# Turning tokens by TensorE transposes in a two-layer cross-attention kernel on one core

## The chip, the core and the metric

The kernel runs on one NeuronCore of a Trainium2 chip. The core has a matrix engine (TensorE, in the profile PE, its weight loads PEld), a vector engine (VectorE, DVE), a scalar engine (ScalarE, ACT), a general engine (GpSimd, POOL) and an engine that issues DMAs (SyncE, SP). TensorE multiplies a stationary operand (at most 128 by 128, loaded first) with a moving one and writes to PSUM, which has eight banks of 128 partitions by 512 fp32 values. [...]

The metric is the device time of one execution in microseconds (us). It is compared as a median over runs.

## The reference

Two layers work on `x` (8 batches, 512 tokens, 256 channels) with a context (8, 512, 128). Each layer adds an attention and then a feed-forward to `x`, each behind a layer norm:

```python
x = x + _L0_xattn_ref(_layernorm(x), ctx, ...)   # causal self-attention + cross-attention, 16 heads of 16
x = x + _L0_ffn_ref(_layernorm(x), ...)          # 1024 wide, rows quantised to 127 steps, ternary weights
x = x + _L1_xattn_ref(_layernorm(x), ctx, ctx, ...)  # cross-attention, 16 heads of 16
x = x + _L1_ffn_ref(_layernorm(x), ...)          # 1024 wide, one scale for the whole tensor and each weight
```

In layer 0, `y` is the sum of a causal attention of the tokens with themselves and an attention of the tokens to the context, projected by one matrix. The last feed-forward quantises its whole input with one scale, `max(|x|) / 127` over all batches, so it can't start before the last batch's layer norm is done.

## The kernel before

**Units.** The attentions are cut into 24 units: causal self-attention (S), cross-attention of layer 0 (C) and cross-attention of layer 1 (X) for each of 8 batches. A unit has 512 queries, 512 keys and 16 heads. Scores, exponentials and value products run in fp32. Scores are made twice: once with queries in rows, from which VectorE takes each row's maximum (`MATMUL pair<-qk`, then `TENSOR_REDUCE mx<-pair`), and once with keys in rows, from which ScalarE makes the exponentials (`MATMUL bank<-qk`, `ACTIVATE p<-bank`). The value products (`MATMUL bank<-p,v`) take these.

**Tilings of the array.** The score products use 48 or 50 rows of a half of the array (48\*128 and 50\*128 in the profile, in pairs side by side; planner mode "rows"). The value products and all projections use 32 columns at a time, four side by side (128\*32, mode "cols"). Some products use the whole array (128\*128, mode "full").

**Token turns.** Before each projection, tokens have to be turned, so that channels lie on partitions. `ln_job` (line 494 on) loads 512 tokens as a tile `xa` of 128 partitions by 4 token blocks by 256 channels, normalises them, and then, for each half `k` of the channels, multiplies four blocks of 128 by 128 with the identity into one PSUM bank. The function `wide` cuts each of these products into four of 32 columns. ScalarE or VectorE copies the bank into `xlt`, from which the query, key and value projections read. There are 16 such layer norms (8 batches of S, 8 of X; units C take the S tokens again), so 32 banks. An fp32 product appears in the trace as two records.

**The last heads.** `last_heads_job` (line 931 on) ends the last unit without the trip through memory that the other units take: the two last groups of heads are copied from their value bank to `ol`, turned to token order (`MATMUL bank<-ident_r,ol`), divided by their sums into `ytok`, and turned back (`MATMUL bank<-ident_r,ytok`). `last_proj_job` makes the last projection, the statistics and the last layer norm from it.

**The last feed-forward's first inputs.** `turn_job` (line 1032 on) turns the first three batches (`TURNED = 3`) of the last feed-forward's input, `y4`, two banks of four blocks each (`MATMUL bank<-ident_r,y`), as soon as the last projection's products are planned; ScalarE copies the banks back over the tile. Batch 0 is then quantised by ScalarE (one half, `ACTIVATE y<-y,magic,sc_x`) and VectorE (the other half) once the scale `sc_x` is known.

**Order.** No loop runs over units. All the work is written as jobs (Python generators), and a planner, `Plan`, keeps a clock for each engine, advances it by a price for each instruction, and picks the next piece of TensorE work: a maximum step, an exponential step, a value step, or a part of a job, by readiness, priority and how much work ScalarE and VectorE still have queued. The order in which instructions are then issued on every engine, on SP's DMA queue and on POOL too, is fixed at build time. Each engine runs its list in that order and waits where a semaphore says so. TensorE's price is this:

```python
def pe(self, cols, mode="full"):
    if mode != self.mode:
        self.clock["pe"] += SWITCH          # 0.165
        self.mode = mode
    self.clock["pe"] += max(cols / 2415, cols / 2165 - 0.08) if mode == "cols" else 0.008 + cols / 2340
```

PSUM banks are handed out by hand. All products go through a wrapper, `Writer` (line 250 on), whose `matmul` makes the first write of a new use of a bank wait for the last readers of the old one. All products are therefore recorded at one line, L259, and the other engines' operations on banks at L241.

Of the kernel before, what the change touches and what calls it, by code (L numbers as in the profile page):

```python
# [16 lines left out]
NB, T, C, CC, H, D, FF = 8, 512, 256, 128, 16, 16, 1024  # L17
P = 128
# [58 lines left out]
class Plan:  # L77
# [39 lines left out]
    def op(self, kind, n, *deps):  # L117
        fixed, rate = RATE[kind]
        return self.run(kind.rstrip("2"), fixed + n * rate, *deps)

    def dma(self, kb, *deps, dims=2, rate=195):
        t = self.run("sp", 0.33 if dims == 2 else 0.65, *deps)
        self.clock["dma"] = max(self.clock["dma"], t + 0.95) + kb / rate
        return self.clock["dma"] + 0.35

    def until(self, *keys):
        while not all(k in self.at for k in keys):
            yield self.now + 0.2
        t = max((self.at[k] for k in keys), default=0.0)
        if t + LAT > self.now:  # L130
            yield t + LAT
        return t

    def take(self, tag):
        ring = self.rings[tag]
        while not ring:
            yield self.now + 0.2
        t = heapq.heappop(ring)
        if t + LAT > self.now:
            yield t + LAT  # L140
        return t
# [108 lines left out]
class Writer(Readers):  # L250
# [5 lines left out]
        self.tc = tc  # L256

    def matmul(self, out, *args, **kw):
        r = self.eng.matmul(out, *args, **kw)  # L259
        name = out.tensor.name  # L260
        for i in self.of[name]:
            if self.last[i][0] != name:
                for reader in self.last[i][1]:
                    self.tc.add_manual_dep(r.ins, reader.name, SYNC, reason="bank")
                self.last[i] = (name, [])
        return r
# [20 lines left out]
def build(tc, A, out):  # L287
    nc = Engines(tc)
# [8 lines left out]
    plan = Plan()  # L297
# [3 lines left out]
    def tile(tag, shape, dtype, name, pool=wp):  # L301
        return pool.tile(shape, dtype, tag=tag, name=name, bufs=BUFS[tag])
# [15 lines left out]
    def wide(out, lhs, rhs, start=True, stop=True):  # L318


        for c in range(0, P, 32):
            nc.tensor.matmul(out[c : c + 32], lhs[:, c : c + 32], rhs, start=start, stop=stop)

    def pe_next(t=None):

        return (plan.now if t is None else t + LAT, 1.0)
# [19 lines left out]
    ident = ident_r.bitcast(F32)  # L346
# [122 lines left out]
    def stats(x, nm):  # L469

        st = wp.tile([P, NT, 6], F32, tag="bnst", name=f"st_{nm}", bufs=3)
        mv = wp.tile([P, NT, 2], F32, tag="bnmv", name=f"mv_{nm}", bufs=3)
        r = wp.tile([P, NT], F32, tag="rstd", name=f"r_{nm}", bufs=3)
        neg = wp.tile([P, NT], F32, tag="nmean", name=f"nm_{nm}", bufs=3)
        for t in range(NT):
            nc.vector.bn_stats(st[:, t, :], x[:, t, :])
            op("dve", C)
            yield plan.now + 0.4
        for t in range(NT):
            nc.vector.bn_aggr(mv[:, t, :], st[:, t, :])  # L480
        te = plan.run("dve", 0.4)
        nc.gpsimd.tensor_scalar(r, mv[:, :, 1], LN_EPS, 0.0, ALU.add, ALU.add)
        nc.gpsimd.tensor_tensor(r, r, mhalf, ALU.pow)
        nc.gpsimd.tensor_scalar(neg, mv[:, :, 0], -1.0, 0.0, ALU.mult, ALU.add)
        te = plan.run("pool", 1.3, te)
        return mv[:, :, 1], neg, r, te

    def normalise(dst, src, nm, r, t):

        nc.gpsimd.tensor_scalar(dst, src, nm[:, t : t + 1], 1.0, ALU.add, ALU.mult)  # L490
        nc.gpsimd.tensor_scalar(dst, dst, r[:, t : t + 1], 0.0, ALU.mult, ALU.add)
        return plan.run("pool", 0.95)

    def ln_job(key, src, nm, n_uses):

        if key[0] == "X":
            yield from until(("x3", key[1]))
        if key == ("S", 0):
            x = first_x
            yield at["x0"] + LAT  # L500
        else:
            yield from take("xa")
            x = tile("xa", [P, NT, C], F32, f"xa_{nm}")
            nc.sync.dma_start(x, src())
            yield dma(512) + LAT
        var, neg, r, te = yield from stats(x, nm)
        yield te
        for t in range(NT):
            if key == ("S", 0):
                at["first"] = nc.vector.tensor_scalar(  # L510
                    x[:, t, :], x[:, t, :], neg[:, t : t + 1], r[:, t : t + 1], ALU.add, ALU.mult
                ).ins.name
                te = op("dve2", C, te)
            else:
                te = normalise(x[:, t, :], x[:, t, :], neg, r, t)
        yield from take("xlt")
        xlt[key] = tile("xlt", [P, 2, T], F32, f"xlt_{nm}")
        uses[key] = [n_uses, 0.0]
        for k in range(2):
            yield pe_next(te)  # L520
            ps, pb = yield from gen_bank()
            for t in range(NT):
                wide(ps[:, t * P : (t + 1) * P], x[:, t, k * P : (k + 1) * P], ident)
            tm = plan.pe(4 * T, "cols")
            tm = evacuate(xlt[key][:, k, :], ps, T, tm)
            give_bank(pb, tm)
        give("xa", tm)
        at[key] = tm
# [402 lines left out]
    def last_heads_job():  # L931
        key = ("X", NB - 1)
        yield from until(("y", *key, 0))
        yt = y_t[key]
        yield from take("rb")
        ytok = tile("rb", [P, T], F32, "ytok").rearrange("p (t h d) -> p t h d", t=NT, d=D)
        for i, G in enumerate((NG - 2, NG - 1)):
            yield from take("oc")
            yield from until(("av", G))
            o = tile("oc", [P, T], F32, f"ol{i}")  # L940
            bank = av_t.pop(G)
            t = evacuate(o, banks[bank], T)
            plan.bank_give("av", bank, t)
            yield pe_next(t)
            ps, pb = yield from gen_bank()
            for k in range(NT):
                nc.tensor.matmul(ps[:, k * P : (k + 1) * P], o[:, k * P : (k + 1) * P], ident, start=True, stop=True)
            t = plan.pe(4 * T)
            give("oc", t)
            ps4 = ps.rearrange("p (t h r) -> p t h r", t=NT, h=4)  # L950
            rz = wp.tile([P, 32], F32, tag="zr", name=f"rz{i}", bufs=2)[:, :16].rearrange("p (t h) -> p t h", t=NT)
            nc.vector.reciprocal(rz, ps4[:, :, :, D])
            plan.run("dve", 0.3, t)
            nc.vector.tensor_tensor(
                ytok[:, :, 4 * i : 4 * i + 4, :], ps4[:, :, :, :D], rz.unsqueeze(3).broadcast_to([P, NT, 4, D]), ALU.mult
            )
            t = op("dve", 256)
            give_bank(pb, t)
        yield pe_next(t)
        ps, pb = yield from gen_bank()  # L960
        for k in range(NT):
            nc.tensor.matmul(
                ps[:, k * P : (k + 1) * P], ytok[:, k].rearrange("p h d -> p (h d)"), ident, start=True, stop=True
            )
        t = plan.pe(4 * T)
        at["yl"] = evacuate(yt[:, 1], ps, T, t)

    def last_proj_job():
# [63 lines left out]
    def turn_job():  # L1032

        yield from until(("acc", 1))
        for b in range(TURNED):
            y = early["y4"][b]
            yield plan.now
            for k in range(2):
                yield pe_next()
                ps = yield from gen_bank()  # L1040
                for t in range(NT):
                    yield pe_next()
                    nc.tensor.matmul(
                        ps[0][:, t * P : (t + 1) * P], y[:, t, k * P : (k + 1) * P], ident, start=True, stop=True
                    )
                    plan.pe(T)
                if k == 0:
                    first = ps
            for k, (bank, i) in enumerate((first, ps)):
                nc.scalar.copy(y[:, 2 * k : 2 * k + 2].rearrange("p t c -> p (t c)"), bank)  # L1050
                give_bank(i, op("act", T))
# [400 lines left out]
    while plan.jobs or a < len(AV_STEPS):  # L1452
# [24 lines left out]
        if any(can.values()):  # L1477
            k = min(urgent)[1] if urgent else "e" if closing and can["e"] else "a" if can["a"] else min((feed[k], k) for k in "me" if can[k])[1]
# [74 lines left out]
    cols = iter(range(64))  # L1553
# [40 lines left out]
    for bs in ((0,), (1,), (2, 3), (4, 5), (6, 7)):  # L1594
# [3 lines left out]
        for f in range(8):  # L1598
            i = 8 * b + n * f
            ps = [banks[2 + i % 6]] if n == 1 else [pairs[1 + f % 3][:, x] for x in range(2)]  # L1600
# [86 lines left out]
    for i in range(2 * NB):  # L1687
# [4 lines left out]
        ps = half_ps.pop(i, None)  # L1692
        if ps is None:
            ps = bias_first(i)

        for j in range(16):
            f, t = (j // 2, j % 2) if i == 0 else (j % 8, j // 8)
# [76 lines left out]
```

## Time and profile before

| | |
|---|---|
| median of 3 runs | 1463.38 us |
| all runs | 1459.09, 1463.38, 1472.07 us |
| span of the profiled execution, first to last instruction | 1458.4 us |
| instructions in it | 36089 |
| mean granted TensorE clock | 0.971 |
| first token turns | 9.16 to 12.57 us |
| last exponentials done; last value product done | 1358.35; 1361.74 us |
| last feed-forward, from its first product | 1377 to 1458 us |

The profile is of one execution; the page shows its span, and its own device time is not listed beside it. The median of the runs is 5.0 us above the span. A line of the groups names the source line, the engine, the operation, output and inputs by the program's names, shapes and the number of instructions; after the bar stand the total busy time in us, the mean of one instruction in ns, and the engine's idle time before them with what ended it. A line of the timeline gives the start in us, the length in us, and the same names; in square brackets stands the idle time of the engine before it.

The stretches of the run, as busy us of each engine with the number of instructions, then the granted clock, the DMA share and GB/s:

```
100.00:400.00 300.00, 291.24 (x3286) 126.17 (x3290) 236.29 (x326) 212.16 (x412) 148.15 (x207) 0.99 0.58 136
400.00:700.00 300.00, 291.66 (x3396) 126.55 (x3393) 249.65 (x364) 219.11 (x411) 160.44 (x239) 0.99 0.64 148
700.00:1000.00 300.00, 288.03 (x3216) 123.52 (x3208) 235.54 (x328) 216.18 (x410) 144.94 (x215) 0.97 0.60 139
1000.00:1340.00 340.00, 324.14 (x2992) 123.35 (x2984) 283.47 (x360) 260.06 (x493) 151.53 (x238) 0.98 0.59 146
1340.00:1380.00 40.00, 36.94 (x213) 19.32 (x212) 13.62 (x42) 24.55 (x46) 9.70 (x18) 0.89 0.26 95
```

The engines in each row are TensorE's products, its weight loads, VectorE, ScalarE and GpSimd.

### The profile page before, as it was taken

What the parts mean: (1) busy time and instruction counts of PE and PEld (TensorE: products, weight loads), DVE (VectorE), ACT (ScalarE), POOL (GpSimd) and SP (SyncE); (2) the same over time, 40 slices, a digit from 0 to 9 for tenths busy, and PEclk for the clock granted to TensorE, in tenths of its full rate; (3) what the DMA queues carried; (4) which work ended last, traced back from release to release, by engine and by line L of the source; (5) the groups of instructions that cost most, each with busy time, mean ns of one, the idle gap of its engine ahead of it and who ended that gap; (6) DMA issues with size and microseconds to landing.
All of it is one profiled execution on the core that took longest, in us unless ns stands there. A gap on an engine that the chain in (4) does not pass through costs nothing. (4 is left out here: it accounts for less than half of the span.)

```text
span 1458.4 us, 36089 instructions
## 1 busy us (share of the span) xinstructions
PE 1374.8 (94%) x14400; PEld 597.5 (41%) x14400; DVE 1142.0 (78%) x1591; ACT 1035.5 (71%) x1904; POOL 681.6 (47%) x1025
## 2 busy tenths in 40 slices
PE   4999999999999999999999999999999998999978
PEld 2443444444444444434344433443333333333527
DVE  4678588697788886898777996689899888766397
ACT  1456767677768867767677777668778795777587
POOL 1463355465455465464653552654455541524332
PEclk8899999999999999999899999999999999999899
DMA  6593565667576755665457655556647657373343
GB/s 126 152 216 76 133 139 125 142 138 182 132 161 150 161 129 141 156 161 126 105 126 155 163 126 132 142 120 160 163 105 169 155 149 196 105 176 110 117 142 116
DMA packets 155612, 207.03 MB, mean 142 GB/s; under 512 B 71940, under 2 KB 74244, under 8 KB 154932
## 3 DMA queue, kind: packets, MB, share of 16 engines
q1 hardware_dynamic: 155444, 204.73, 58.0%
q8 instruction: 113, 1.85, 0.5%
q14 instruction: 55, 0.45, 0.1%
HBM read 68.15 MB, written 47.43 MB: 79 GB/s over the span
## 5 line engine op out<-in xcount | busy, mean ns | idle before, releaser
L241 DVE TENSOR_REDUCE mx<-pair 128x2 f32<-128x1024 f32 (+3 forms) x768 | 808.9, 1086 | 210.7 <-PE pair L259 194.6
L241 ACT ACTIVATE p<-bank 128x512 f32<-128x512 f32 (+1 forms) x1408 | 712.0, 587 | 232.7 <-PE bank L259 224.8
L259 PE MATMUL bank<-p,v 128*32 128x512 f32 (+3 forms) x3072 | 371.7, 563 | 2.9 <-DVE mrow L241 1.3
L259 PE MATMUL bank<-qk 50*128 50x512 f32 (+3 forms) x1536 | 337.6, 433 | 16.2 <-ACT p L241 8.0
L259 PE MATMUL pair<-qk 48*128 48x512 f32 (+3 forms) x1536 | 325.5, 438 | 25.7 <-DVE mx L241 11.8
L259 PEld LDWEIGHTS bank<-qk 50*128 50x128 f32 x1536 | 159.6, 190 | 215.7 <-ACT p L241 142.9
L259 PEld LDWEIGHTS pair<-qk 48*128 48x128 f32 x1536 | 148.0, 191 | 171.5 <-DVE mx L241 83.4
L384 POOL TENSOR_SCALAR qkt<-qkt 128x512 fp32r<-128x512 f32 x92 | 57.1, 621 | 164.1 <-ACT qkt L241 157.5
L241 ACT ACTIVATE qkt<-bank,qk_bias 128x512 f32<-128x512 f32 x96 | 66.6, 693 | 81.0 <-PE bank L259 65.4
L409 POOL TENSOR_TENSOR qkt<-qkt 128x512 fp32r<-128x512 f32 x92 | 118.8, 1291 | 7.7
L259 PEld LDWEIGHTS bank<-p,v 128*32 128x32 f32 x3072 | 70.9, 109 | 114.6 <-issue 85.9
L384 POOL TENSOR_SCALAR mhl<-mx 128x32 fp32r<-128x32 f32 x48 | 11.8, 245 | 171.3 <-DVE mx L241 164.8
L883 POOL TENSOR_TENSOR yt<-oc,rb 128x512 f32<-128x512 f32 x31 | 39.8, 1283 | 73.3 <-DMA rb<-scrz 50.9
L259 PE MATMUL pair<-mask,ident 64*128 64x128 bf16 (+2 forms) x768 | 58.0, 226 | 6.9 <-DVE mx L241 4.7
L259 PE MATMUL bank<-ident,mask 64*128 64x64 bf16 (+1 forms) x768 | 52.7, 206 | 3.7 <-ACT p L241 1.2
L259 PEld LDWEIGHTS <-ident 64*128 64x128 bf16 x768 | 26.1, 97 | 71.0 <-issue 52.8
L259 PEld LDWEIGHTS <-mask 64*128 64x128 bf16 x768 | 25.8, 96 | 69.3 <-issue 61.0
L241 ACT COPY v<-bank 128x512 f32<-128x512 f32 x44 | 26.2, 596 | 39.4 <-PE bank L259 39.1
L241 ACT COPY ev<-bank 128x512 f32<-128x512 f32 x56 | 33.5, 598 | 17.9 <-PE bank L259 17.9
L241 DVE SCALAR_TENSOR_TENSOR h<-bank,so,bc_l_b 128x512 f32<-128x512 f32 x64 | 45.3, 741 | 0.9 <-PE bank L259 0.7
L241 ACT ACT_TABLE_LOAD x34 | 43.6, 1283 | 1.9 <-PEq L1762 0.7
L1189 POOL TENSOR_SCALAR h<-h,sh 128x1024 f32<-128x1024 f32 x32 | 36.0, 1125 | 17.7 <-DVE sh L241 15.2
(230 smaller groups left out, 1686.4 us busy)
## 6 DMA issues: line engine op xcount, KB each, us to landing
qk<-qkt SPq DMA_DIRECT2D x288, 256.0 KB
scro<-ev SPq DMA_DIRECT2D x94, 256.0 KB
oc<-scro SPq DMA_DIRECT2D x47, 256.0 KB
rb<-scrz SPq DMA_DIRECT2D x47, 256.0 KB
x_d<-xb SPq DMA_DIRECT2D x15, 512.0 KB
xa_s<-in_x SPq DMA_DIRECT2D x8, 512.0 KB
xb<-in_x SPq DMA_DIRECT2D x8, 512.0 KB
xr<-x_d SPq DMA_DIRECT2D x16, 256.0 KB
```

What stands on the lines that cost most here:

```text
L241: r = f(*args, **kw)
L259: r = self.eng.matmul(out, *args, **kw)
L384: nc.gpsimd.tensor_scalar(dst, src, 1.0, 0.0, ALU.mult, ALU.add)
L409: nc.gpsimd.tensor_tensor(dst, full, high.bitcast(F32), ALU.subtract)
L883: nc.gpsimd.tensor_tensor(y, o, rb, ALU.mult)
L1189: nc.gpsimd.tensor_scalar(ht, ht, s[:, t - t0 : t - t0 + 1], MAGIC, ALU.mult, ALU.add)
```

## The change

Wherever a block of 128 by 128 was multiplied by the identity to turn it (token turns, the last heads both ways, the last feed-forward's first inputs), the kernel calls TensorE's transpose with the same operands instead. The token turns, which were four products of 32 columns for each block, become one transpose of 128 by 128 for each block. `Writer` gets a `transpose` next to `matmul`, with the same waits for banks. The planner's prices change with it: a bank of four blocks is priced at 512 columns in place of 2048, and a single block in `turn_job` at 128 in place of 512. The token turns keep the mode "cols" in the planner's price. The other products with the identity, among them the row maxima's, the one that adds the residual in `last_proj_job` and `all_max`, stay.

```diff
--- before.py
+++ after.py
@@ -256,7 +256,12 @@
         self.tc = tc
 
     def matmul(self, out, *args, **kw):
-        r = self.eng.matmul(out, *args, **kw)
+        return self.writes(out, self.eng.matmul(out, *args, **kw))
+
+    def transpose(self, out, *args):
+        return self.writes(out, self.eng.transpose(out, *args))
+
+    def writes(self, out, r):
         name = out.tensor.name
         for i in self.of[name]:
             if self.last[i][0] != name:
@@ -520,8 +525,8 @@
             yield pe_next(te)
             ps, pb = yield from gen_bank()
             for t in range(NT):
-                wide(ps[:, t * P : (t + 1) * P], x[:, t, k * P : (k + 1) * P], ident)
-            tm = plan.pe(4 * T, "cols")
+                nc.tensor.transpose(ps[:, t * P : (t + 1) * P], x[:, t, k * P : (k + 1) * P], ident)
+            tm = plan.pe(T, "cols")
             tm = evacuate(xlt[key][:, k, :], ps, T, tm)
             give_bank(pb, tm)
         give("xa", tm)
@@ -944,8 +949,8 @@
             yield pe_next(t)
             ps, pb = yield from gen_bank()
             for k in range(NT):
-                nc.tensor.matmul(ps[:, k * P : (k + 1) * P], o[:, k * P : (k + 1) * P], ident, start=True, stop=True)
-            t = plan.pe(4 * T)
+                nc.tensor.transpose(ps[:, k * P : (k + 1) * P], o[:, k * P : (k + 1) * P], ident)
+            t = plan.pe(T)
             give("oc", t)
             ps4 = ps.rearrange("p (t h r) -> p t h r", t=NT, h=4)
             rz = wp.tile([P, 32], F32, tag="zr", name=f"rz{i}", bufs=2)[:, :16].rearrange("p (t h) -> p t h", t=NT)
@@ -959,10 +964,8 @@
         yield pe_next(t)
         ps, pb = yield from gen_bank()
         for k in range(NT):
-            nc.tensor.matmul(
-                ps[:, k * P : (k + 1) * P], ytok[:, k].rearrange("p h d -> p (h d)"), ident, start=True, stop=True
-            )
-        t = plan.pe(4 * T)
+            nc.tensor.transpose(ps[:, k * P : (k + 1) * P], ytok[:, k].rearrange("p h d -> p (h d)"), ident)
+        t = plan.pe(T)
         at["yl"] = evacuate(yt[:, 1], ps, T, t)
 
     def last_proj_job():
@@ -1040,10 +1043,8 @@
                 ps = yield from gen_bank()
                 for t in range(NT):
                     yield pe_next()
-                    nc.tensor.matmul(
-                        ps[0][:, t * P : (t + 1) * P], y[:, t, k * P : (k + 1) * P], ident, start=True, stop=True
-                    )
-                    plan.pe(T)
+                    nc.tensor.transpose(ps[0][:, t * P : (t + 1) * P], y[:, t, k * P : (k + 1) * P], ident)
+                    plan.pe(P)
                 if k == 0:
                     first = ps
             for k, (bank, i) in enumerate((first, ps)):
```

## The prediction

> **What bounds the kernel now.** I read the page's busy table and slices first, then the groups of TensorE instructions by shape, then TensorE's timeline round single token turns, and last the waits and the timeline of the end.
>
> ```profile
> PE 1374.8 (94%) x14400; PEld 597.5 (41%) x14400; DVE 1142.0 (78%) x1591; ACT 1035.5 (71%) x1904; POOL 681.6 (47%) x1025
> PE   4999999999999999999999999999999998999978
> PEclk8899999999999999999899999999999999999899
> ```
>
> TensorE is in the top tenth in nearly every slice, at a granted clock of 0.9 or more after the first 70 us. Busy time of pipelined products overlaps, so I asked who waits for whom. The waits say the same: ScalarE's exponentials waited 224.8 us for TensorE and VectorE's maxima 194.6 us, while TensorE's own longest totals are 16.5 us (for VectorE's maxima) and 9.8 us (for the exponentials). From some 30 us to 1340 us the kernel is bound by TensorE's stream, and what leaves that stream shortens the run, unless it uncovers another wait. The chain that ended last reaches back to 1377 us only and says nothing of this middle.
>
> The groups that change, by shape (mean ns of one record stands after the bar's comma):
>
> ```profile
> L259 PE MATMUL bank<-ident_r,xa_s 128*32 128x128 f32 x512 | 18.3, 291 | 9.2 <-DVE xa_s L241 9.2
> L259 PE MATMUL bank<-ident_r,xa_x 128*32 128x128 f32 x512 | 18.1, 285 | 0.0
> L259 PE MATMUL bank<-ident_r,y 128*128 128x128 f32 x48 | 5.5, 275 | 0.0
> L259 PE MATMUL bank<-ident_r,ol 128*128 128x128 f32 x16 | 2.2, 281 | 0.0
> L259 PE MATMUL bank<-ident_r,ytok 128*128 128x128 f32 x8 | 1.1, 275 | 0.0
> ```
>
> An fp32 product is two records: 16 layer norms, two halves, 16 products of 32 columns make 1024 records. The token turns are 36.4 us of busy time, everything else that changes is 8.8 us.
>
> **Pitch of a token turn.** Not the busy time but the distance to the next group's start is what a group costs. TensorE's timeline (start, us, group):
>
> ```profile
> 510.00 1.06 PE L259 MATMUL bank<-p,v 128*32 128x512 f32 x8
> 511.00 0.23 PE L259 MATMUL bank<-ident,mask 64*128 64x64 bf16 x4
> ...
> 512.18 1.07 PE L259 MATMUL bank<-xlt_s,w_Sq 128*32 128x512 f32 x8
> 513.06 1.06 PE L259 MATMUL bank<-ident_r,xa_x 128*32 128x128 f32 x32
> 514.05 0.73 PE L259 MATMUL pair<-qk 48*128 48x512 f32 x4
> 514.71 1.08 PE L259 MATMUL bank<-ident_r,xa_x 128*32 128x128 f32 x32
> 515.61 1.04 PE L259 MATMUL bank<-xlt_s,w_Sq 128*32 128x512 f32 x8
> ```
>
> The group at 513.06 costs 0.99 us (a row-tiled score group, 48*128, follows), the one at 514.71 costs 0.90 (a 32-column group follows). A 32-column group of the same work costs 512.18 to 513.06 = 0.88 before another 32-column group and 510.00 to 511.00 = 1.00 before a row-tiled one. So leaving one tiling of the array for another costs 0.12 us.
>
> I read the timeline round all turns. Apart from the two at the start (9.16 us), there are 30; 11 have a 32-column group before them and 2 behind; all other neighbours are row-tiled.
>
> **Pitch after.** A turn becomes four 128 by 128 transposes. No transpose stands in this trace. The nearest rows are full-array fp32 products of the same size:
>
> ```profile
> 350.07 0.49 PE L259 MATMUL bank<-ident_r,l1w1s 128*128 128x128 f32 x2
> 350.49 0.26 PE L259 MATMUL pair<-mask,ident 64*128 64x128 bf16 x4
> ...
> 1369.40 5.54 PEld L259 LDWEIGHTS bank<-ident_r,y 128*128 128x128 f32 x48
> ```
>
> 48 weight loads of 128 fp32 columns take 5.54 us, 0.115 each, with the products beside them. I take one load and one product for a transpose, bound by the load: 4 x 0.115 = 0.46. The fixed part: two records cost 0.42 between row-tiled groups (350.07 to 350.49); less 2 x 0.115 that leaves 0.19 for the first load and the way out. A turn then costs 0.65.
>
> - Between row-tiled groups: 0.99 - 0.65 = 0.34 saved; 30 x 0.34 = 10.2 us.
> - With a 32-column group before: the change of tiling is new, 11 x 0.12 = 1.3 us lost. Behind: 2 x 0.09 (0.90, not 0.99, was paid before) = 0.2 lost.
> - Sum 8.7 us. TensorE has little idle time between 100 and 1340 us (busy 291 of 300 us in such windows), so I let 8 us through: about a tenth is eaten where the next group waits for VectorE or ScalarE anyway.
>
> Bounds of the price. Low: an fp32 product takes its pair of records, 0.23 us; a quarter of it would be 0.0575, 4 x 0.0575 + 0.19 = 0.42, saving 0.57 x 30 - 1.5 = 15.6 us. High: nothing overlaps and each transpose shows the full 275 ns of one record: 4 x 0.275 + 0.19 = 1.29, a loss of 0.30 x 30 + 1.5 = 10.5 us. I take the load's rate because 48 loads of this very shape were streamed so, and neither end was seen.
>
> The Trainium skill speaks against the change here ("TensorE: Matmul & The Clock Gate", Part 4): a transpose takes about 275 ns in a kernel, and does not count as activity for the clock gate. By its price the sum would be the loss of the high end, some 10 us. The trace can't show a transpose; what it shows of the clock is 0.97 to 0.99 over the windows from 100 to 1340 us, and a turn of 0.65 us comes once in some 45 us.
>
> The same rule of exclusion decides the tiling: the skill ("TensorEngine Tiling (Array Packing)", Gotcha 2) says that column tiling and fp32 transposes exclude each other. No run here shows it.
>
> **Start.** The first two turns reach from 9.16 to 12.57 us, where the first query product starts. VectorE's last token tile ends at 10.08, and ScalarE's copy of half 0 starts at 11.16. With transposes half 0 is done some 0.3 us after 10.08, half 1 0.46 later: the query product could start near 11.0, 1.5 earlier. Behind it lie the second half's weights, whose DMA lands near 14.7, and from 19 to 27 us the stacking DMAs of queries and keys. Between 0 and 1.5 I take 1.0.
>
> **End.** After the last value product (1361.7) the chain runs through two head turns and the token-order turn, then the projection, the statistics and the input scale:
>
> ```profile
> 1363.52 1.05 PE L259 MATMUL bank<-ident_r,ol 128*128 128x128 f32 x8
> 1364.41 1.02 PE L259 MATMUL bank<-xb,ident_r 128*128 128x512 f32 x2
> ...
> 1374.73 1.07 ACT L241 COPY y<-bank 128x512 f32<-128x512 f32 x2 [0.71 <-PE bank L259]
> 1375.82 1.28 ACT L241 ACT_TABLE_LOAD   x1
> ```
>
> Two of the turns (the second head group, and the one from token order back) lie on it: 8 records to 4, 0.46 each, 0.9 together. Then ScalarE waits 0.64 and 0.71 us for the y turns before it copies them; the table load (1.28) and the first quantising step (1377.22) are behind those copies, while the scale that it needs is ready at 1376.1. The 24 y turns fall from 5.5 to 2.8 us, the copies close up, and the step then starts when the scale is there: 1.1 more. Sum 2.0; bounds 0 (the copies are late for another reason) and 2.5.
>
> **What moves.** The program's order is made by a planner from prices. A token turn's price falls from 0.866 (2048 columns) to 0.212 (512), 32 times, 20.9 us of planned TensorE time, against my 0.65 a piece. So the plan, close to the chip before (0.866 to 0.90-0.99), becomes optimistic at these points, and everything behind them, on all engines and on SP's and POOL's queues (loads, stacking, row DMAs, normalising), may stand in another order. No added wait, DMA or instruction is visible in the edit. I price the new order at 0, and give it 6 us either way: as the waits of TensorE in the middle sum to about 45 us, that is an eighth of them.
>
> **Sum.** 8 + 1 + 2 = 11 us from the span of 1458.4: 1447.4. The median of the runs is 1463.4, 5.0 above the span; added back, 1452.
>
> **Rivals.**
> 1. *Transposes run at the quarter price.* 15.6 + 1.5 + 2.5 = 19.6, so 1444. For it: the change's own prices assume it. Against: the load's rate of 0.115.
> 2. *The new order adds TensorE waits.* The plan thinks TensorE earlier than it is, puts score groups before VectorE has freed their banks (today 30 such waits, 16.5 us, and 18 for the exponentials, 9.8), and the in-order stream stops. With the 45 us up by half, 1452 + 22 = 1474, slower. It decides from 11 us of added waits on (no gain left), and passes 1% slower from 26. For it: nothing in the edit re-tunes the planner's other constants. Against: banks and buffers are as before and the plan knows real bank releases through the same rules.
> 3. *A transpose is no faster than the product* (the high end): 10.5 lost in the turns and about 1 at the end: 1475.
> 4. *Nothing is gained because VectorE takes over*: it is at 78%, so 11 us less leave it at 79%; I give it no share of its own.
>
> **Numbers.** Forecast (order within 6 us, price near the load's rate) 0.52, range 1446 to 1458. Rival 1: 0.22. Rival 2: 0.18. Rival 3: 0.08. Range 1438 (rival 1 with 6 us from the order) to 1469 (inside rival 2). A measurement of this kernel tells about 1% (14.6 us) from no change. Faster by more (under 1448.7): rival 1 nearly whole, and a quarter of the forecast: 0.34. Slower by more (over 1478): half of rival 2 and a little of rival 3: 0.11. Between: 0.55.
>
> **What would show it.** TensorE records fall from 14400 to 13468 if a transpose is one record (896 + 12 + 24 fewer). Turn pitch in the timeline: 0.65 right, 0.42 rival 1, over 1.0 rival 3. TensorE's waits for maxima and exponentials: unchanged right, up by over 10 us rival 2. The first query product near 11 us, the y copies without gaps. The forecast is wrong if turns are short and the span does not fall: then the waits must have grown by as much.

## The result and the profile after

The changed kernel takes 1524.21 us (median of 4 runs, 1516.70 to 1533.17) against 1462.34 us before: 1.0417 times the time before, 95% interval 1.0364 to 1.0469. The forecast was 1452 us in a range of 1438 to 1469. It missed, on the wrong side.

The page of the kernel after: busy table, then the slices of TensorE and of its granted clock.

```profile
PE 1397.8 (92%) x13468; PEld 587.9 (39%) x13468; DVE 1139.6 (75%) x1576; ACT 1041.9 (68%) x1919; POOL 678.9 (45%) x1025
PE   5999999999998998998999999899899999899878
PEclk8899999999998998998999999999899999899899
```

There are 13468 TensorE records, as forecast: 932 fewer, since a transpose leaves one record. Yet TensorE's busy time has grown by 23.0 us and its idle time from 83.6 to 126.6 us (span less busy). The slices show both: eights stand now in the middle of the TensorE row, and more of them than before in that of the clock. The mean granted clock of the profile fell from 0.971 to 0.939.

The transposes themselves, by shape, and TensorE's timeline round two turns:

```profile
L262 PE MATMUL bank<-ident_r,xa_s 128*128 128x128 f32 x64 | 11.0, 305 | 9.4 <-DVE xa_s L241 9.2 <-ACT p L241 0.2
L262 PE MATMUL bank<-ident_r,xa_x 128*128 128x128 f32 x64 | 10.9, 303 | 0.7 <-POOL xa_x L496 0.7
L262 PE MATMUL bank<-ident_r,y 128*128 128x128 f32 x24 | 2.9, 275 | 0.0
L262 PE MATMUL bank<-ident_r,ol 128*128 128x128 f32 x8 | 1.3, 280 | 0.0
L262 PE MATMUL bank<-ident_r,ytok 128*128 128x128 f32 x4 | 0.6, 272 | 0.0
```

```profile
66.90 0.48 PE L259 MATMUL bank<-qk 50*128 50x512 f32 x2
67.31 0.66 PE L262 MATMUL bank<-ident_r,xa_s 128*128 128x128 f32 x4
67.90 0.85 PE L259 MATMUL bank<-p,v 128*32 128x384 f32 x8
68.68 0.30 PE L259 MATMUL bank<-ident_r,mhl 64*16 64x64 f32 x8
68.91 0.66 PE L262 MATMUL bank<-ident_r,xa_s 128*128 128x128 f32 x4
69.50 0.64 PE L259 MATMUL bank<-p,v 128*32 128x256 f32 x8
```

A turn costs 67.31 to 67.90, 0.59 us, where the forecast had 0.65 and the old one 0.99. The busy time of all that was changed fell from 45.2 (36.4 + 8.8) to 26.7 us. So the turns are not the loss: without them TensorE's busy time grew by 23.0 + 18.5 = 41.5 us, at a lower clock, and its idle time by 43.0.

TensorE's waits (us in total, times, longest), three of before first, then the longest after:

```profile
PE pair L259 <- DVE mx L241: 16.5, 30, 1.6
PE bank L259 <- DMA qk<-mrow: 4.6, 2, 2.7
PE bank L259 <- DVE am L241: 1.8, 1, 1.8
```

```profile
PE pair L259 <- DVE mx L241: 32.6, 48, 2.3
PE bank L259 <- DMA qk<-mrow: 12.9, 5, 7.2
PE bank L259 <- ACT p L241: 12.7, 29, 1.6
PE pair L259 <- DMA qk<-qkt: 11.3, 6, 7.3
PE bank L259 <- DVE am L241: 9.5, 3, 5.4
```

Waits for VectorE's maxima doubled, from 16.5 us to 32.6; those for the DMAs of the maxima rows rose from 4.6 to 12.9, those for `am` (the maxima by which a feed-forward quantises) from 1.8 to 9.5. One of the waits for rows, on SP's queue (its DMA issues, with the time they held the queue) and on TensorE:

```profile
583.33 5.19 SPq L612 DMA_DIRECT2D qk<-qkt  x6
588.62 1.46 SPq L746 DMA_DIRECT2D qk<-mrow  x2
```

```profile
586.62 0.38 PE L259 MATMUL pair<-qk 48*128 48x256 f32 x2
594.24 1.41 PE L259 MATMUL bank<-qk 50*128 50x512 f32 x2 [7.23 <-DMA qk<-mrow]
```

Six stacking DMAs of 256 KB stand on SP ahead of the two 16 KB DMAs with the maxima rows, without which the next exponential group can't start. TensorE stands for 7.23 us. The stretches round it (busy us and instructions of TensorE, its loads, VectorE, ScalarE and GpSimd, then granted clock, DMA share, GB/s) show what follows:

```profile
582.10:585.50 3.40, 3.40 (x72) 2.46 (x72) 2.89 (x5) 1.59 (x4) 1.04 (x1) 1.00 0.29 68
585.50:588.90 3.40, 1.41 (x14) 0.40 (x12) 2.24 (x4) 0.58 (x1) 0.00 (x0) 0.99 1.00 193
588.90:602.50 13.60, 8.26 (x62) 3.94 (x62) 2.45 (x2) 4.45 (x8) 0.51 (x2) 0.50 0.80 154
602.50:606.00 3.50, 3.50 (x46) 1.69 (x46) 2.40 (x6) 3.03 (x8) 0.31 (x1) 1.00 0.23 81
```

After a stretch of 3.4 us in which TensorE worked for 1.41, its clock is halved for 13.6 us, and its products take about twice as long in them (eight value products of 512 columns took 1.93 us in a half-clock piece of before, at 1354.57 us, and 1.06 outside it, at 1349.28). A wait can thus be paid twice. Over the run, the clock stood at one half in 12 pieces and 85.3 us before, in 27 pieces and 184.6 us after; this is called half-clock time below. TensorE's busy time inside these pieces was 74.0 us before and 159.6 after. At half speed, half of the 85.6 us added is stretch: 42.8 us, which accounts for the 41.5.

### The profile page after: what moved, and what is told of

The parts are those of the page before. It is cut to its first block, busy times and chain, and to the rows that moved or that the text cites. A ratio compares the mean times of both kernels' runs of the same rounds, so it can differ in the third digit from the quotient of the medians.

```text
span 1524.4 us, 34236 instructions
## 1 busy us (share of the span) xinstructions
PE 1397.8 (92%) x13468; PEld 587.9 (39%) x13468; DVE 1139.6 (75%) x1576; ACT 1041.9 (68%) x1919; POOL 678.9 (45%) x1025
## 4 chain that ended last, share of the span: by engine, by line
PE 63%; DVE 11%; DMA 10%; ACT 7%; POOL 4%; issue 3%; SPq 2%; POOLq 0%; ACTq 0%; DVEq 0%
PE bank L259 49%; PE pair L259 12%; DVE mx L241 5%; DMA qk<-qkt 4%; ACT p L241 3%; DMA qk<-mrow 2%; SPq L612 2%; DVE gmax L241 2%; PE bank L262 1%; DMA hqt<-hq 1%; ACT L241 1%; DVE am L241 1%; ACT h L241 1%; DMA w_Vs<-in_wv 1%; DMA rb<-scrz 1%
## 5 line engine op out<-in xcount | busy, mean ns | idle before, releaser
L259 PE MATMUL pair<-qk 48*128 48x512 f32 (+3 forms) x1536 | 335.9, 450 | 47.5 <-DVE mx L241 24.2
L259 PE MATMUL bank<-qk 50*128 50x512 f32 (+3 forms) x1536 | 345.5, 440 | 34.1 <-DMA qk<-mrow 12.9
L259 PEld LDWEIGHTS pair<-qk 48*128 48x128 f32 x1536 | 152.8, 197 | 190.6 <-DVE mx L241 94.4
L241 ACT COPY ev<-bank 128x512 f32<-128x512 f32 x67 | 40.0, 596 | 21.1 <-PE bank L259 16.8
L241 ACT ACT_TABLE_LOAD x34 | 43.6, 1283 | 12.7 <-DVE h L241 11.4
L241 ACT CAST mrow<-bank 16x256 fp32r<-16x256 f32 x88 | 27.4, 356 | 20.5 <-PE bank L259 20.0
```

What stands on the lines that cost most here:

```text
L241: r = f(*args, **kw)
L259: return self.writes(out, self.eng.matmul(out, *args, **kw))
```

## The experiments

Two theories stood against each other. **O**: the new order of the engines' lists costs the time, by waits and by the clock that halves behind them. **T**: the transposes themselves cost it, by changes of the array's tiling or because they do not count as activity for the clock. In all kernels below that keep the old prices, the lists of every engine have the order of the kernel before (in the run on the end alone, up to the last heads). Each kernel is told by its difference from before or after.

**Instruction and price apart.** Transposes everywhere, at the old prices (the second hunk stands for both places in `last_heads_job`):

```diff
-            tm = plan.pe(T, "cols")
+            tm = plan.pe(4 * T, "cols")
...
-            t = plan.pe(T)
+            t = plan.pe(4 * T)
...
-                    plan.pe(P)
+                    plan.pe(T)
```

> All transposes of the change, but the planner's old prices (2048 columns for a turned bank, 512 for a single block), so every engine's list keeps the order of the kernel before. Theory O (the new order of the lists costs the time, by waits of TensorE and the clock that halves behind them): the forecast of the prediction holds, 1452 us (1440 to 1460), TensorE's half-clock time near the 85 us of before. Theory T (the transposes themselves cost it, by changes of tiling or because they do not count for the clock): 1510 or more, half-clock time near the 185 us of after.

Measured: 1469.78 us (10 runs), 1.0033 of before (1.0005 to 1.0062); half-clock time 127.6 us in its profile. With the old order all but some 6 of the 62 us are gone, so T falls as the main cause. But the forecast's gain isn't there either: the run is slightly slower than before.

The reverse, old products at the new prices (before, with 512 and 128 columns in the planner):

> The old products with the identity, but the change's prices (512 and 128 columns), so the lists have the order of the changed kernel. Theory O: slower than the changed kernel, since each of the 32 turned banks costs some 0.4 us more: 1524 + 12 = 1536 (1520 to 1550). Theory T: the time of before, 1462, within 1%.

Measured: 1535.11 us, 1.0497 (1.0452 to 1.0542). The plan that the new prices make is 5% slower, with not one transpose in it. TensorE has the very products of before in this run's profile, and its busy time is 40.2 us longer (1415.0 against 1374.8), its idle time 34.1 us. The transposes then take 10.9 us off it (to 1524.21). That this is close to the 11 us of the forecast is in part luck: the intervals of the two kernels overlap, and their difference is known to some 10 us only.

**Is the price too low, or is any other order worse?** A token turn priced near what it costs, in two ways: 0.46 us in the full mode, with 0.165 for each change of mode, and 0.580 us in its old mode:

```diff
-            tm = plan.pe(T, "cols")
+            tm = plan.pe(1060)
...
-            tm = plan.pe(T, "cols")
+            tm = plan.pe(1400, "cols")
```

> The change with a price for a token turn close to what was measured: 1060 columns in the full mode (0.46 us, plus 0.165 for each change of mode) in place of 512 in the mode of 32 columns. Theory O in its form O1 (the order is bad because the price is too low): 1455 (1445 to 1470). Form O2 (the planner's other constants fit the old prices alone, and any other order loses): 1480 to 1530. Theory T: about 1524.

> The change with a token turn priced in its own mode at 1400 columns, 0.580 us, which is the pitch measured after (0.59), in place of 0.212. Form O1: 1455 to 1475. Form O2: 1475 to 1530, like the 1481 us of the honest price in the full mode.

Measured: 1481.09 us, 1.0134 (1.0088 to 1.0179), and 1517.63 us, 1.0367 (1.0321 to 1.0414). A price that agrees with the chip does not bring the time back; with the better of two such prices the kernel still loses 1.3%, with the other 3.7%.

The same question without the change: the products of before, their price moved by 5% up or down (2150 and 1950 columns in place of 2048).

> The kernel before, with the price of a turned bank raised by 5% (2150 columns, 0.913 us, in place of 0.866), so that the planner makes another order with a price no worse than the old one (measured pitch 0.90 to 1.06). Form O1 (order is bad only where prices are far from the chip): within 1% of before, 1455 to 1475. Form O2 (the other constants fit one order, and any other order loses some per cent): 1475 to 1530.

> The kernel before, with the price of a turned bank lowered by 5% (1950 columns, 0.821 us). Form O1: within 1% of before, 1455 to 1480. Form O2: 1475 to 1530.

Measured: 1486.78 us, 1.0147 (1.0101 to 1.0193), and 1486.64 us, 1.0159 (1.0116 to 1.0201). No work was added or taken away, and both directions lose some 1.5%. Form O2 holds: the order of before is a good one that none of the five others tried reached, and how far an order falls (1.3 to 5.0%) doesn't follow from how wrong its price is.

The order is not all that a price moves. The planner also chooses by its clocks whether ScalarE or VectorE copies a bank, so with other prices some copies change engine: ScalarE has 1904 instructions before and 1919 after, 1913 and 1917 in the two runs just told, 1923 in the run priced in the full mode (1.3% lost) and 1906 in the one priced at 0.580 (3.7% lost). The number moved doesn't follow the loss, so the split of the copies is not likely to be the cause, but no run holds it fixed under a new order. Where this text says "order", it means the whole plan, this split with it.

**Why the old order gains nothing from shorter turns.** With equal order, each TensorE group of e1 can be set against its twin of before. Where a row-tiled group stands ahead of a turn, the group behind it mostly starts 0.42 us earlier, where a 32-column group does, 0.29 (the forecast had 0.34 and 0.22). In the 10 stretches with no half clock in either profile (20 turns), 7.0 us are won at the groups behind the turns, and 2.6 us of them are left 10 us later. One such place, first before, TensorE's groups from a turn on and two of ScalarE's:

```profile
1124.42 2.12 PE L259 MATMUL bank<-ident_r,xa_x 128*32 128x128 f32 x64
1126.46 0.50 PE L259 MATMUL pair<-qk 48*128 48x512 f32 x2
1128.24 1.09 ACT L241 ACTIVATE jq<-h 128x1024 bf16<-128x1024 f32 x1
1129.22 2.24 PE L259 MATMUL bank<-w_Wo,yt 128*32 128x256 f32 x32
1129.30 2.08 ACT L241 ACTIVATE p<-bank 128x512 f32<-128x512 f32 x4
1131.40 0.51 PE L259 MATMUL bank<-qk 50*128 50x512 f32 x2
```

and the same in e1:

```profile
1135.54 0.55 PE L262 MATMUL bank<-ident_r,xa_x 128*128 128x128 f32 x3
1136.33 0.77 PE L262 MATMUL bank<-ident_r,xa_x 128*128 128x128 f32 x5 [0.24 <-POOL xa_x L496]
1137.03 0.50 PE L259 MATMUL pair<-qk 48*128 48x512 f32 x2
1139.37 1.09 ACT L241 ACTIVATE jq<-h 128x1024 bf16<-128x1024 f32 x1
1140.21 0.64 PE L259 MATMUL bank<-w_Wo,yt 128*32 128x256 f32 x8
1140.42 2.07 ACT L241 ACTIVATE p<-bank 128x512 f32<-128x512 f32 x4
1141.08 1.50 PE L259 MATMUL bank<-w_Wo,yt 128*32 128x256 f32 x24 [0.24 <-ACT p L241]
1142.52 0.50 PE L259 MATMUL bank<-qk 50*128 50x512 f32 x2
```

Counted from the start of the turns, the next score pair comes at 1.49 us in place of 2.04, so 0.55 is won (and 0.24 is already lost inside the turns, to the normalising on GpSimd). The projection `w_Wo` starts at 4.67 in place of 4.80, stops for 0.24 behind ScalarE's exponentials, and the next group starts at 6.98 in both. ScalarE's groups stand at 3.83 and 4.88 in e1, at 3.82 and 4.88 before: its list is as long as it was, works without a break, and holds the path here.

What was kept, and more, was lost to the clock. In e1's profile TensorE's busy time inside half-clock pieces is 114.0 us against 74.0; half of the difference, 20 us, is stretch, more than the 18.5 us that the transposes took out. Nor is it one profile: the mean granted clock is 0.961 over e1's 10 runs (standard error 0.001), 0.9695 over 19 runs of before (0.001). To see whether transposes don't count for the clock or merely leave TensorE emptier, e1 was run with each token transpose issued twice:

```diff
             for t in range(NT):
-                nc.tensor.transpose(ps[:, t * P : (t + 1) * P], x[:, t, k * P : (k + 1) * P], ident)
+                for _ in range(2):
+                    nc.tensor.transpose(ps[:, t * P : (t + 1) * P], x[:, t, k * P : (k + 1) * P], ident)
```

> As the run with transposes at the old prices (1470 us, median clock 0.962 over its runs, against 0.970 before at the same order), but every token transpose is issued twice into the same place, so that a turn takes about 1.05 us of TensorE again. Theory E (the time that shorter turns free is not used, TensorE waits instead, and more windows become sparse enough to halve the clock): clock back to 0.968 to 0.972 and 1458 to 1468 us. Theory N (transposes do not count as activity for the clock): clock 0.962 or lower and 1470 to 1485 us, since twice as many uncounted operations stand there.

Measured: 1465.58 us, 1.0017 (0.9997 to 1.0037), a turn at 1.02 us, clock 0.967 (mean of 10 runs, standard error 0.001), half-clock time 99.0 us. Twice the transposes raise the clock by 0.006 rather than lower it, to just under E's 0.968 (before, beside this run: 0.9685). N falls. In time the two runs are not told apart (their intervals overlap); that 14 us of useless TensorE work cost nothing is the point.

The other direction, the products of before made twice:

```diff
+            for _ in range(2):
                 for t in range(NT):
                     wide(ps[:, t * P : (t + 1) * P], x[:, t, k * P : (k + 1) * P], ident)
```

> The kernel before with every product of a token turn made twice into the same place, at the old price and order, so that a turn takes some 1.87 us in place of 1.00 and TensorE has 30 x 0.87 = 26 us more to do (28 with the start). If TensorE's stream is the path at the turns, as the prediction had it: 1463 + 26 = 1490 (1482 to 1495). If other engines are level with it there (theory E, by which 0.41 us less a turn gained nothing): clearly less, 1465 to 1480, with a clock no lower than before.

Measured: 1487.00 us, 1.0196 (1.0154 to 1.0238), against 1460.74 beside it: 26 us more, with the clock at 0.970 (mean of 4 runs; 0.971 beside it). Longer turns are paid in full, so theory E's "clearly less" was wrong: TensorE's stream is the path as soon as it gets longer. It is level with the others, not behind them. In this order a turn that lengthens delays all engines; one that shortens meets ScalarE and VectorE at their old times, as at the place shown.

**The end alone.** Transposes in the last heads and `turn_job`, at the change's prices; token turns as before.

> Transposes only in the last heads and the last feed-forward's first inputs, with the change's prices there; the token turns stay products at the old price, so the lists are those of before up to the last heads. All theories: 1460, some 2 us under before (0 to 2.5), by the prediction's term for the end.

Measured: 1461.16 us, 0.9993 (0.9971 to 1.0016). A gain as small as expected can't be told from none. The trace tells it better: from the end of the last value product to the first product of the last feed-forward it was 15.45 us before (1361.73 to 1377.18), is 13.88 in this run (1362.60 to 1376.48) and 13.85 in the changed kernel (1429.32 to 1443.17).

**The row DMAs.** In after and, as a control, in before, the two DMAs of each maxima row go out by ScalarE's queue:

```diff
-            nc.sync.dma_start(
+            nc.scalar.dma_start(
                 qk_t[n % NQK].bitcast(F32)[64 * c + 48 : 64 * c + 50, :, 0], row.bitcast(F32)[8 * c : 8 * c + 8]
```

> The changed kernel, its lists as they are, but the two small DMAs of each maxima row go out through ScalarE's queue and not behind others on SP's. TensorE waited 12.9 us for them after, 4.6 before (one wait of 7.23 us at 587 us, where six stacking DMAs of 256 KB stood ahead on SP). If the place on SP's queue is the cause of these waits: 1524 less 8 to 13 and less some us of half clock behind them, 1500 to 1515. If the rows themselves are late or ScalarE pays as much for issuing: 1520 to 1535.

> Control for the last: the kernel before with the same move of the row DMAs to ScalarE's queue. Waits for rows are only 4.6 us there: 1455 to 1475, within 1% of before.

Measured: 1524.85 us for after with the move (1.0431, 1.0370 to 1.0493), 1475.27 us for before with it (1.0106, 1.0073 to 1.0140), just outside what was expected. TensorE's waits for rows do fall in the first, from 12.9 to 3.5 us, but the waits for exponentials rise from 12.7 to 18.4 (the profile is of this kernel's fastest run, 1510.94 us):

```profile
PE pair L259 <- DVE mx L241: 31.6, 45, 3.8
PE bank L259 <- ACT p L241: 18.4, 35, 2.7
...
PE bank L259 <- DMA qk<-mrow: 3.5, 3, 1.6
```

The move costs before 14.5 us, and after nothing that the spread of its runs (1510.94 to 1529.37) would show. It may take something off the new order and put something of its own on; that was not shown. What the place on SP's queue is worth stays open.

## Why the prediction was wrong

- **The price of a transpose: right.** One load and one product for each, one every 0.12 us (24 in 2.9 us), 0.59 for a turn (forecast 0.65). Rivals 1 (0.42) and 3 (over 1.0) fall. The Trainium skill ("TensorE: Matmul & The Clock Gate", Part 4) gives about 275 ns for a transpose of 128 by 128 in a kernel, for bf16. For fp32 here the length of one record agrees (275 ns for `y`), the distance from one to the next does not (0.12 us).
- **The end: near.** 1.6 us in place of 2.0. **The start: nothing in place of 1.0.** The first two turns took 2.23 us in place of 3.41, and the first query product started at 11.45 us in place of 12.57. But it took 3.64 us in place of 1.95: the record of the clock begins, at full speed, at 15.43 us in place of 12.56 (in the other runs between 11.8 and 15.9, so the change need not be the reason). TensorE's first score group then waited 7.3 us for the stacking DMAs, as before, and started at 28.06 us, 0.8 later than before.
- **"So I let 8 us through": wrong for the order it was meant for.** It rested on busy 291 of 300 us. At the old order about a third came through, and the lower clock took more back. In the new order, which is not fitted to the turns, the transposes do take off time (1535.11 to 1524.21, 10.9 us, give or take 10).
- **"I price the new order at 0, and give it 6 us either way": the step that failed.** The new order without the transposes costs 72 us (1535.11 against 1463.56). It should have been the largest term; the 6 us rested on nothing but an eighth of the waits. Rival 2 named the mechanism, planned time too early and VectorE's banks not yet free, but gave it 0.18 and half of 45 us. The idle time grew by 43.0, nearly the whole 45 again; the waits for VectorE's maxima and for the exponentials, the prediction's own sign of rival 2 from 10 us on, are 19.0 us of that (16.1 and 2.9). Most of the rest are waits that it didn't name, those for the rows' DMAs (8.3) and `am` (7.7) ahead.
- **The clock was taken as given.** The prediction read the clock as 0.9 or more after the first 70 us, though its clock row has two more eights, near 700 and 1350 us. The forecast and rival 2 priced waits at their length. Their second half, 99 us more at half clock, stood in no sum; of the 66 us between the two profiled spans, 41.5 less the 18.5 saved are busy time stretched by it, 43.0 are idle.
- **Against rival 2 the prediction argued that the plan knows bank releases by the same rules.** It knows its own times for them. The runs with a 5% price show that even small shifts in these lose some 1.5%.

What stays open is why some orders lose 1.3% and others 5.0%; the five tried show the spread, not its rule. No kernel tried beats the one before beyond its interval.

## What to carry to other kernels

In a kernel whose lists are laid out at build time by a planner, an edit of an instruction is two edits: what the chip does, and the order that the planner makes of its price. Measure them apart, by keeping the old price under the new instruction and the new price under the old one, and don't count on a new order to be as good as the old one before it is measured: all five here were worse. A share of busy time of 97% does not say that time saved on that engine is time saved: try a longer and a shorter version of the piece, because the two can cost differently.

## What the runs showed of the hardware that was not expected

- **The clock falls after short stretches of thin work.** The clock changes in steps of 3.41 us. For each such window at full clock, the columns that TensorE streamed were summed (those of an fp32 record twice), weighted with the share of the array that its tile takes. As a full stream counts that of eight value products of 512 columns on a quarter of the array, which take 0.88 us. It is a rough measure. After: of 29 windows below 0.6 of a full stream 22 were followed by half clock, of 30 between 0.6 and 0.8 five, of 329 above none. Before: 10 of 18, 1 of 26, 1 of 354 (this one at 0.8). A half-clock piece lasted 3.4 to 13.7 us in the middle of the run. The Trainium skill ("TensorE: Matmul & The Clock Gate", Part 1) has the clock fall after an idle window of some 3.4 us, and also tells of a kernel in which short idle times between groups of products were enough. The second is what is seen here: in 23 of the 27 windows no gap was longer than 2.3 us, in 16 none longer than 1.2.
- **Transposes do not starve the clock here.** None of the 27 windows of the kernel after that were followed by half clock held a token turn (two of 19 did in e1), and d1 shows a higher clock with twice as many.
- **Three changes of tiling cost about the same.** Leaving the 32-column tiling for the whole array or for a row-tiled group both cost some 0.12 us (a 32-column group of 0.88 us takes 1.00 in front of either). A turn by transposes mostly takes 0.49 us in front of another turn, which is four times 0.12, and 0.59 in front of another tiling.
